# A four-layer graph network on one core: layer 2 by two levels of Strassen, its adjacency applied in PSUM, and weights fetched from DRAM in every turn

## The chip, the core and the metric

The kernel runs on one core of a Trainium2 chip. TensorE multiplies, with its results in PSUM; VectorE (DVE), ScalarE (ACT) and GpSimd (POOL) do the elementwise work; SP issues DMAs. All data are 32-bit floats. The metric is the time of one execution on the device in microseconds (us), as the median of the runs. Lower is better.

## The reference

There are 128 graphs of 128 nodes with 512 features, and a weighted adjacency matrix for each graph. Four layers follow each other, each of the form `x = layernorm(x + layer(x))`:

```python
# layer 0: A1 = A + I, normalised on both sides by d = rowsum(A1)**-0.5
out = relu(einsum('bnm,bmf,fc->bnc', An, x, kernel) + bias)
# layer 1: one weight for each node, from scores summed over the neighbours, softmax over the nodes
w = softmax(sum((q @ k.T) / 8 * adj, -1), axis=1);  out = w * v        # q, k, v = x @ W
# layer 2: W has 512 x 1024 elements, one half for x, one for the mean of the neighbours
agg = einsum('bij,bjf->bif', adj, x) / maximum(deg, 1e-6)
out = relu(einsum('bnf,of->bno', concatenate([x, agg], 2), W))
# layer 3: normalised A1 as in layer 0
out = An @ (x @ W + b)
```

## The kernel before

The work goes in 32 turns `t` of four graphs (`G = 4`, `NT = 32`). A product of the four graphs with a 512 x 512 weight is done by one level of Strassen: the rows are split by graph pairs `r` (graphs 0 and 2 against 1 and 3), the inner and the output dimension in halves, and the seven products are called B11, T1, T2, B21, B22, T3 and T4. Each weight tile holds its four blocks and the four sums that Strassen needs, made once at the start (`weight_sums`); the sums of the left operand are made each turn (`left_sums`, on GpSimd). `project` runs the seven products for one pair of graph rows after another, keeps partial results in PSUM banks that ScalarE copies between products (`copied`), and ends with `fin`, which adds onto `x` on VectorE. Its last product, T4, is put off as a *tail* (`finish_tails`) so that other work can stand before it.

A turn's path: `load`, `prep_rows` and `prep_turn` fetch the adjacency and make its two transposed forms `anT` (layers 0 and 3) and `arT` (layers 1 and 2). `l0_agg` multiplies x with `anT` (`aggregate`) and ScalarE copies the result to `agg0`; `l0_out` projects. `l1_turn` brings x, transposed, to `xT1`; `l1_out` makes v, q and k together (320 columns, tile `p_v`); `l1_scores`, `l1_softmax` and `l1_add` weigh v by graph: the weights come back to all partitions through a small TensorE transpose, `p_ws`, and VectorE then adds weighted v onto x. `l2_turn` brings the new x, transposed, to `xT2`; `l2_agg` multiplies x with `arT` to `agg2`; `l2_out` projects both halves, `xT2` with `w2x_sb` and `agg2` with `w2a_sb`, into the same products. `l3_agg`, `l3_bias` and `l3_out` end the turn, and `store` writes x.

The transposing (`turn_x`) in all turns but the first and the last goes through DRAM: four DMAs write x to a scratch tile (`xT2s` or `xT1s`), eight read it back in another order (`xT2y`, `xT1y`), and VectorE transposes blocks of 32 x 32. In the first and last turns TensorE transposes (`turn_on_tensor`). Normalisation is in `norm_stats`: mean and variance by VectorE's statistics instructions, the power -0.5 on GpSimd, and the scaling on ScalarE; layer 3 uses `norm_last`, in which ScalarE sums the values and their squares.

All the calls are recorded by `Plan`, and `emit` (line 323, the line that nearly every instruction of the profile shows) writes the instructions in the order that `schedule` chose. `estimate` gives each operation a duration, `Op.last` is its due time, found backwards from those that need it, and `run` lets each engine take the ready operation that is due first. TensorE keeps the order in which the calls were written, with `hooks` and `tails` to interleave them:

```python
        l0_out(t, {T2: [lambda: l2_agg(u, 0)], B21: [lambda: l2_agg(u, 1)]})
    tails.append(lambda: l1_turn(t))
    prep(t + 1)
    l2_out(u)
```

with `u = t - 1`: layers 0 and 1 of turn `t` run beside layers 2 and 3 of turn `u`. All weights stay in SBUF. SP issues the DMAs in one queue, in order.

Of the kernel before, what the change touches and what calls it, by code (L numbers as in the profile page):

```python
# [29 lines left out]
B11, T1, B21, B22, T2, T3, T4 = range(7)  # L30

# [95 lines left out]
class Plan:  # L127
# [8 lines left out]
    TRIALS = 100  # L136
# [62 lines left out]
    def schedule(self):  # L199
        number = {op: i for i, op in enumerate(self.ops)}  # L200
        for (_, tag, bufs), tiles in self.tags.items():
            used = []
            for t in sorted((t for t in tiles if t.ops), key=lambda t: number[t.ops[0]]):
                if len(used) == bufs:
                    old = used.pop(min(range(bufs), key=lambda i: number[used[i].ops[-1]]))
                    assert number[old.ops[-1]] < number[t.ops[0]], (tag, bufs)
                    for op in t.ops:
                        if op.preds.isdisjoint(t.ops):
                            op.preds.update(old.ops)
                used.append(t)  # L210
        now = 0
        for op in self.ops:
            assert all(number[p] < number[op] for p in op.preds)
            for p in op.preds:
                p.succs.append(op)
            if op.engine == "tensor":
                op.last = now
                now += op.dur
        for op in reversed(self.ops):
            due = min([s.last - self.hop(op, s) for s in op.succs], default=now)  # L220
            op.last = min(op.last, due - op.dur)
        done = self.run(number)
        tried = set()
        for _ in range(self.TRIALS):
            free, moves = 0, []
            for op in self.ops:
                if op.engine == "tensor":
                    gap, free = op.start - free, op.end
                    if gap > 100:
                        moves += [(-gap, number[op], n, op) for n in range(2)]  # L230
            moves = [m for m in sorted(moves) if m[1:3] not in tried]
            if not moves:
                break
            tried.add(moves[0][1:3])
            kept = [(op, op.start, op.end, op.after, op.last) for op in self.ops]
            self.press(moves[0][3], -moves[0][0], moves[0][2])
            again = self.run(number)
            if max(op.end for op in again) < max(c[2] for c in kept) - 20:
                done, tried = again, set()
            else:  # L240
                for op, start, end, after, due in kept:
                    op.start, op.end, op.after, op.last = start, end, after, due
        return done

    def press(self, op, gap, delay):


        while op.preds:
            late = max(op.preds, key=lambda p: p.end + self.hop(p, op))
            if delay and op.engine not in ("tensor", "sync"):  # L250
                ready = late.end + self.hop(late, op)
                for other in self.ops:
                    if other.engine == op.engine and other.start < op.start and other.end > ready + 20:
                        other.last = max(other.last, op.last + 100)
            op = late
            if op.engine == "tensor":
                break
            if not delay:
                op.last -= gap

    def run(self, number):
        queue = {e: [] for e in self.ENGINES}
        waiting = {op: len(op.preds) for op in self.ops}
        for op in self.ops:
            op.after = None
        free, bus, port, owner = dict.fromkeys(self.ENGINES, 0), 0, 0, None
        pe = [op for op in self.ops if op.engine == "tensor"]
# [4 lines left out]
        while len(done) < len(self.ops):  # L272
            best = None
            for e in self.ENGINES:
                q = queue[e]
                if e == "tensor":
                    q = [c for c in q if c[2] is pe[0]]
                if not q:
                    continue
                q = [(max(c[0], port if c[2].port else 0),) + c[1:] for c in q]  # L280
# [18 lines left out]
            if op.port:  # L299
                ready = max((p.end + self.hop(p, op) for p in op.preds), default=0)  # L300
                if e == "gpsimd" and owner is not None and owner.engine == "vector" and ready < port + self.CLOSE:
                    op.after = owner
                port, owner = op.end, op
# [4 lines left out]
            if e == "tensor":  # L308
                pe.pop(0)
            done.append(op)  # L310
            for s in op.succs:
                waiting[s] -= 1
                if not waiting[s]:
                    queue[s.engine].append((max(p.end + self.hop(p, s) for p in s.preds), number[s], s))
# [32 lines left out]
def estimate(engine, method, args, kw):  # L347
# [5 lines left out]
    if method == "dma_start":  # L353
        size = max(int(np.prod(v.shape)) if isinstance(v, bass.AP) else v.idx.size * 32 * len(v.quads) for v in args)
        return 470, Plan.LAND + size / 60, size, False
    if engine == "scalar":
        return (380 if method == "activation" else 160) + 0.83 * n, 0, 0, False
# [5 lines left out]
    return 160 + (1.12 if len(both) > 1 else 1.04) * n, 0, 0, len(both) > 1  # L363
# [3 lines left out]
def kernel(  # L367
# [19 lines left out]
    xp = Pool(nc, ctx.enter_context(tc.tile_pool(name="xp", bufs=4)), 4)  # L387
    ap = Pool(nc, ctx.enter_context(tc.tile_pool(name="ap", bufs=2)), 2)
    tp = Pool(nc, ctx.enter_context(tc.tile_pool(name="tp", bufs=4)), 4)
    sp = Pool(nc, ctx.enter_context(tc.tile_pool(name="sp", bufs=4)), 4)  # L390
# [23 lines left out]
    def weight(src, name, queue, turned=False):  # L414


        w = const.tile([P, 2, 7, H], FP, tag=name, name=name)
        for h in range(2):
            to = w[:, :, 2 * h:2 * h + 2].rearrange("p c j m -> p c (j m)")
            if turned:  # L420
                for b in range(Q):
                    queue.dma_start(to[b * K:(b + 1) * K], src.rearrange("(b h c k) m -> h b k c m", b=Q, h=2, c=2)[h][b])
            else:
                queue.dma_start(to, src.rearrange("(h c p) m -> h p c m", h=2, c=2)[h])
        return w

    def weight_sums(w, eng):
# [3 lines left out]
        eng.tensor_tensor(w[:, :, T4], w[:, :, B21], w[:, :, T2], ALU.subtract)  # L431

# [14 lines left out]
    w0_sb = weight(w0, "w0_sb", nc.sync)  # L447
# [12 lines left out]
    w2x_sb = weight(w2T[0:F, :], "w2x_sb", nc.sync, turned=True)  # L460
    w2a_sb = weight(w2T[F:2 * F, :], "w2a_sb", nc.sync)
    w3_sb = weight(w3, "w3_sb", nc.sync)
# [6 lines left out]
    def prep_rows(t):  # L469
# [3 lines left out]
        nc.vector.tensor_reduce(deg, a, AX.X, ALU.add)  # L473
        dh = sp.tile([P, G], FP, tag="dh", name=f"dh_{t}")
        nc.vector.tensor_scalar(dh, deg, 1.0, None, ALU.add)
        d = sp.tile([P, G], FP, tag="d", name=f"d_{t}")
# [12 lines left out]
    def prep_tiles(t):  # L489
        st["anT", t] = ap.tile([P, G, P], FP, tag="anT", name=f"anT_{t}", bufs=3)  # L490
        st["arT", t] = ap.tile([P, G, P], FP, tag="arT", name=f"arT_{t}", bufs=2)
# [92 lines left out]
    def project(name, t, parts, fin, hooks=None, after=lambda: None, pairs=(0, 1), seeds=None, fold=None):  # L584
# [14 lines left out]
        def product(p, k, fresh=False):  # L599
            with nc.unit():  # L600
                for q in pairs:
                    for i, (left_, w) in enumerate(parts):
                        for c in range(2):
                            nc.tensor.matmul(p[:, q - pairs[0], :], operand(left_, k)[:, q, c, :], w[:, c, k, :],
# [5 lines left out]
        def block(tag):  # L610
            return tp.tile([P, 2, H], FP, tag=tag, name=f"{tag}_{name}_{t}", bufs=2)[:, 0:n]
# [54 lines left out]
    def norm_last(name, t, r, pairs):  # L666

        z = st["x", t]
        qs = slice(pairs[0], pairs[-1] + 1)
        sm, nm, sq, rstd, nmr = (sp.tile([P, 2], FP, tag=f"last{i}", name=f"last{i}_{t}_{r}", bufs=2) for i in range(5))  # L670
        for q in pairs:
            row = tp.tile([P, F], FP, tag="row", name=f"row_{t}_{r}_{q}", bufs=1)
            nc.scalar.activation(row, z[:, 2 * q + r, :], AF.Copy, accum_out=sm[:, q:q + 1])
        nc.scalar.mul(nm[:, qs], sm[:, qs], -1.0 / F)
        for q in pairs:
            row = tp.tile([P, F], FP, tag="row", name=f"square_{t}_{r}_{q}", bufs=1)
            nc.scalar.activation(row, z[:, 2 * q + r, :], AF.Square, bias=nm[:, q:q + 1], accum_out=sq[:, q:q + 1])
        nc.gpsimd.tensor_scalar(rstd[:, qs], sq[:, qs], 1.0 / F, LN_EPS, ALU.mult, ALU.add)
        nc.gpsimd.tensor_tensor(rstd[:, qs], rstd[:, qs], nhalf[:, qs], ALU.pow)
        if (t, pairs[0]) != (last, 1):  # L680
            nc.gpsimd.tensor_tensor(nmr[:, qs], nm[:, qs], rstd[:, qs], ALU.mult)
        for q in pairs:
            zg = z[:, 2 * q + r, :]
            if (t, q) == (last, 1):
                nc.vector.tensor_scalar(zg, zg, nm[:, q:q + 1], rstd[:, q:q + 1], ALU.add, ALU.mult)
            else:
                nc.scalar.activation(zg, zg, AF.Identity, bias=nmr[:, q:q + 1], scale=rstd[:, q:q + 1])
            if t == last:
                nc.sync.dma_start(out[t * G + 2 * q + r], zg)

    def norm_stats(name, t, r, pairs):
        if name == "o3" and (t, r, pairs[-1]) != (last, 1, 1):
            return norm_last(name, t, r, pairs)
# [10 lines left out]
        mr = sp.tile([P, 2], FP, tag="mr", name=f"mr{name}_{t}_{r}")  # L704
# [8 lines left out]
        nc.gpsimd.tensor_tensor(mr[:, qs], mv[:, qs, 0], rstd[:, qs], ALU.mult)  # L713
        nc.scalar.mul(nmr[:, qs], mr[:, qs], -1.0)
# [160 lines left out]
    def l2_agg(t, r):  # L875
        if r == 0:
            left("agg2", t)
# [152 lines left out]
```

## Time and profile before

| | |
|---|---|
| median of 3 runs | 2443.24 us (2443.18 to 2443.28) |
| profiled execution | 2442.89 us, its span 2441.1 us |
| granted TensorE clock | 0.999 |
| DMA traffic | 238.88 MB in the hardware queue, 37.5% of 16 engines' time |

Busy time of each engine, its share of the span, and what it is made of:

| engine | busy us | share | largest groups |
|---|---|---|---|
| TensorE | 2426.6 | 99% | products of layers 0 and 3 (`p_o<-w_sb`), of layer 2 (`w2x_sb`, `w2a_sb`), of layer 1 (`p_v`), aggregations (`p_agg`) |
| VectorE | 1365.1 | 56% | statistics 246, additions onto x, transposes of blocks |
| ScalarE | 1212.1 | 50% | copies of `p_agg` 227, scaling of x |
| GpSimd | 1156.4 | 47% | sums of left operands, powers |

One line of a group reads: line, engine, operation, output and input tiles, shapes, count, then busy us, mean ns of one, and idle time before them with what ended it. The granted clock is the share of full speed that the throttle let TensorE have. The chain of waits is followed back from the last instruction: each step names what released it.

### The profile page before, as it was taken

How to read it: one execution, taken by the hardware profiler on the slowest of the kernel's cores; microseconds unless marked ns; L12 is line 12 of the kernel's file. 1: busy time of each engine (PE TensorE's matmuls, PEld its weight loads, DVE VectorE, ACT ScalarE, POOL GpSimd, SP SyncE). 2: the span in 40 equal slices, each digit the busy share in tenths (PEclk: the TensorE clock that was granted, in tenths of full speed). 3: DMA queues.
4: the chain of work that ended last, by engine and by line, in shares of the span. 5: the costliest groups of instructions: out<-in, count | busy, mean ns of one | idle time of the engine just before them, and what ended most of it. 6: DMA issues, size and time to landing. Idle time of an engine off the chain costs nothing.

```text
span 2441.1 us, 35406 instructions
## 1 busy us (share of the span) xinstructions
PE 2426.6 (99%) x12460; PEld 2088.7 (86%) x12460; DVE 1365.1 (56%) x2847; ACT 1212.1 (50%) x2569; POOL 1156.4 (47%) x1516
## 2 busy tenths in 40 slices
PE   9999999999999999999999999999999999999998
PEld 7888888888888888888888888888888888888887
DVE  5655655555555655656565555556555555655545
ACT  5444544555445454455544554444555445454445
POOL 5353545545454444544444553545445454444442
PEclk9999999999999999999999999999999999999999
DMA  5243333443434434244333444343442434433220
GB/s 177 51 107 95 77 105 103 118 114 73 112 87 125 117 74 104 84 124 117 90 88 99 110 117 108 76 108 94 122 120 66 112 82 126 117 81 97 61 78 35
DMA packets 393264, 241.14 MB, mean 99 GB/s; under 512 B 140416, under 2 KB 358016, under 8 KB 393088
## 3 DMA queue, kind: packets, MB, share of 16 engines
q1 hardware_dynamic: 393088, 238.88, 37.5%
q8 instruction: 99, 1.62, 0.3%
q14 instruction: 77, 0.63, 0.1%
HBM read 126.62 MB, written 112.20 MB: 98 GB/s over the span
## 4 chain that ended last, share of the span: by engine, by line
PE 97%; POOL 1%; DVE 1%; ACT 1%; issue 0%; DMA 0%; POOLq 0%; ACTq 0%; DVEq 0%
PE p_o L323 63%; PE p_v L323 19%; PE p_agg L323 14%; PE p_sc L323 1%; DVE x L323 0%; POOL xT1s L323 0%; POOL w_sb L323 0%; ACT xT L323 0%; ACT agg L323 0%; PE p_ws L323 0%; PE p_w L323 0%; ACT x L323 0%; DMA ana<-in_adj_dram 0%; POOL w2a_sb L323 0%; ACT xT2y L323 0%
## 5 line engine op out<-in xcount | busy, mean ns | idle before, releaser
L323 PE MATMUL p_o<-w_sb,agg 128*128 128x256 f32 x2048 | 476.8, 380 | 0.8 <-DVE x L323 0.5
L323 PEld LDWEIGHTS p_o<-w_sb,agg 128*128 128x128 f32 x2048 | 381.6, 190 | 51.7 <-DVE x L323 0.9
L323 ACT COPY agg<-p_agg 128x512 f32<-128x512 f32 (+1 forms) x415 | 226.7, 554 | 376.6 <-PE p_agg L323 376.6
L323 DVE SCALAR_TENSOR_TENSOR x<-p_o,x 128x512 f32<-128x512 f32 (+1 forms) x130 | 88.7, 683 | 405.2 <-PE p_o L323 402.4
L323 PE MATMUL p_v<-wv_sb,xT 128*128 128x320 f32 x1024 | 307.2, 433 | 0.0
L323 PE MATMUL p_o<-w2x_sb,xT 128*128 128x256 f32 x1024 | 263.1, 379 | 0.5 <-ACT xT L323 0.5
L323 PE MATMUL p_o<-w2a_sb,agg 128*128 128x256 f32 x1024 | 262.8, 379 | 0.0
L323 PEld LDWEIGHTS p_agg<-anT,x 128*128 128x128 f32 x2048 | 243.6, 192 | 11.8 <-DVE anT L323 0.4
L323 PEld LDWEIGHTS p_v<-wv_sb,xT 128*128 128x128 f32 x1024 | 189.7, 190 | 71.2 <-issue 0.2
L323 PE MATMUL p_agg<-anT,x 128*128 128x128 f32 x2048 | 244.2, 275 | 0.2 <-DVE anT L323 0.2
L323 ACT COPY p_o<-p_o 128x512 f32<-128x512 f32 (+1 forms) x196 | 110.7, 565 | 255.8 <-PE p_o L323 255.8
L323 PE MATMUL p_v<-wv_sb,xT1s 128*128 128x320 f32 x768 | 228.3, 433 | 1.1 <-POOL xT1s L323 1.0
L323 PEld LDWEIGHTS p_o<-w2x_sb,xT 128*128 128x128 f32 x1024 | 194.2, 190 | 30.5 <-ACT xT L323 1.0
L323 PEld LDWEIGHTS p_o<-w2a_sb,agg 128*128 128x128 f32 x1024 | 194.6, 190 | 26.5
L323 ACT ACTIVATE x<-x,nmro,rstdo 128x512 f32<-128x512 f32 x256 | 198.0, 808 | 4.1
L323 PE MATMUL p_o<-w2x_sb,xT2s 128*128 128x256 f32 x768 | 197.3, 379 | 2.0 <-DVE xT2s L323 2.0
L323 PE MATMUL p_o<-w2a_sb,agg2s 128*128 128x256 f32 x768 | 197.1, 379 | 0.0
L323 PEld LDWEIGHTS p_v<-wv_sb,xT1s 128*128 128x128 f32 x768 | 145.6, 190 | 59.5 <-POOL xT1s L323 2.6
L323 PE MATMUL p_o<-w_sb,agg0s 128*128 128x256 f32 x768 | 176.4, 379 | 0.0
L323 POOL TENSOR_TENSOR xT1s<-xT 128x512 f32<-128x512 f32 x32 | 40.7, 1273 | 277.4 <-DVE xT L323 250.4
L323 PE MATMUL p_o<-w_sb,agg3s 128*128 128x256 f32 x744 | 171.2, 379 | 0.6 <-POOL agg3s L323 0.6
L323 DVE BATCH_NORM_STATS2 bno<-x 128x6 f32<-128x512 f32 x258 | 164.8, 679 | 3.4
(143 smaller groups left out, 4024.3 us busy)
## 6 DMA issues: line engine op xcount, KB each, us to landing
x<-in_x_dram SPq DMA_DIRECT2D x31, 1024.0 KB, 5.4
out_dram<-x SPq DMA_DIRECT2D x31, 1024.0 KB, 5.7
xT2s<-x SPq DMA_DIRECT2D x120, 256.0 KB, 2.5
xT2y<-xT2s SPq DMA_DIRECT2D x240, 128.0 KB, 3.4
xT1s<-x SPq DMA_DIRECT2D x120, 256.0 KB, 2.5
xT1y<-xT1s SPq DMA_DIRECT2D x240, 128.0 KB, 3.4
sa<-ana SPq DMA_DIRECT2D x120, 128.0 KB, 3.1
ya<-sa SPq DMA_DIRECT2D x120, 128.0 KB, 3.9
```

Source lines behind the costliest of these rows:

```text
L323: op.ins = getattr(getattr(self.nc, op.engine), method)(*[v.real() if isinstance(v, Ref) else v for v in args], **{k: v.real() if isinstan ...
```

## The change

**Layer 2.** Instead of aggregating x first, the kernel multiplies x with both halves of the weight, as one 512 x 1024 product, by two levels of Strassen: 7 x 7 products of one matmul each (128 rows, 128 inner, 256 columns). The first level is over pairs of graphs, inner chunks and columns within a half; the second over graph rows, inner halves and the two halves of W. The sums of the left operand are made by `l2_turn` and `inner_sums` (two of them on VectorE as the transposes arrive, the others mostly on GpSimd). The products go in four passes (`PASSES`), interleaved by `AT`; each pass collects into `v` (the x half) and `y` (the half to be aggregated) on VectorE and ScalarE. Then, for each graph, ScalarE copies `v` into a PSUM bank, one matmul of 512 columns with `arT` adds the aggregated `y` onto it (`p_2g`), and VectorE adds the positive part to x, with the sum over features as a by-product. `l2_agg` and `l2_both` are gone.

**Weights.** Four tiles `wb_sb`, `wa_sb`, `wc_sb` and `wz_sb` hold layer 2's weights and sums; `wz_sb` is also the place of the weights of layers 0 and 3. Their three versions are written to DRAM at the start (`keep`) and fetched in seven pieces each, three times in a turn (`fetch`); each piece waits until the products that read the one before it are done.

**Normalisation.** Layers 1 and 2 take their means from the by-products of the additions, and the squares on ScalarE (`norm_last`), instead of VectorE's statistics. Layer 0 makes `nmr` in one VectorE instruction for one of GpSimd and one of ScalarE.

**Buffers.** x has three buffers for four, the left operands and small tiles three for four, `arT` three for two.

**Order.** The search over `press` is gone. `run` now also lets TensorE choose by due time, gives buffers out as it goes, and takes two tables that are written out in the file: `EARLY` shifts the due time of operations named by engine, tile and number within a turn (366 entries), and `MOVED` names operations that go to another engine (`move`): additions between VectorE and GpSimd, copies and scalings from ScalarE to VectorE.

```diff
+PASSES = (B11,), (B21, T2), (T1, T3), (B22, T4)
+AT = 0, 0.5, 7, 9
...
-            due = min([s.last - self.hop(op, s) for s in op.succs], default=now)
-            op.last = min(op.last, due - op.dur)
...
+            due = min([s.last - self.hop(op, s) for s in op.succs + then[op]], default=now)
+            op.last = min(op.last, due - op.dur) - 100 * EARLY.get(keys[op], 0)
+        return self.run(number)
...
-                if e == "tensor":
-                    q = [c for c in q if c[2] is pe[0]]
+                q = [(r,) + c[1:] for c in queue[e] for r in (ready(c[0], c[2]),) if r is not None]
...
-    xp = Pool(nc, ctx.enter_context(tc.tile_pool(name="xp", bufs=4)), 4)
+    xp = Pool(nc, ctx.enter_context(tc.tile_pool(name="xp", bufs=3)), 3)
...
+    def fetch(name):
+        def piece(k):
+            nc.sync.dma_start(wz_sb[:, k], st[name, "kept"][:, k])
+
+        for k in ORDER[:-1]:
+            piece(k)
...
-        nc.gpsimd.tensor_tensor(mr[:, qs], mv[:, qs, 0], rstd[:, qs], ALU.mult)
-        nc.scalar.mul(nmr[:, qs], mr[:, qs], -1.0)
+        nc.vector.scalar_tensor_tensor(nmr[:, qs], mv[:, qs, 0], -1.0, rstd[:, qs], ALU.mult, ALU.mult)
...
+            def product(p, k, fresh=False):
+                with nc.unit():
+                    for i, j in enumerate(js):
+                        nc.tensor.matmul(p[:, i], ops[j][k], w[:, k, i], start=(fresh and i == 0), stop=True,
+                                         skip_group_check=True)
...
+                p = ps_b.tile([P, F], FP, tag="pb", name=f"p_2g_{t}_{g}")
+                nc.scalar.copy(p, v[:, r, q].rearrange("p i m -> p (i m)"))
+                nc.tensor.matmul(p, st["arT", t][:, g, :], y[:, r, q].rearrange("p i m -> p (i m)"), start=False, stop=True,
+                                 skip_group_check=True)
+                nc.vector.scalar_tensor_tensor(z[:, g, :], p, 0.0, z[:, g, :], ALU.max, ALU.add,
+                                               accum_out=st["sm", t][:, 2 * r + q:2 * r + q + 1])
...
-            l0_out(t, {T2: [lambda: l2_agg(u, 0)], B21: [lambda: l2_agg(u, 1)]})
+            fetch("w0d")
+            l0_out(t)
...
+        fetch("w2d")
         tails.append(lambda: l1_turn(t))
         prep(t + 1)
         l2_out(u)
+        fetch("w3d")
+        l1_out(t, {})
         if t < last:
             l0_agg(t + 1)
-        l1_out(t, {})
+        finish_tails()
+        l1_scores(t)
         l3_agg(u)
-        l1_scores(t)
+        l1_softmax(t)
         l3_bias(u)
-        l3_out(u, {B11: [lambda: l1_softmax(t)], T2 if t < last else T1: [lambda: l1_add(t)]})
-        if t < last:
-            l2_turn(t)
-
-    l2_both(last, 0)
...
+        l3_out(u, {B11: [lambda: l1_add(t)]})
+        l2_turn(t, turn_x if t < last else turn_on_tensor)
+
+    fetch("w2d")
+    l2_out(last)
+    fetch("w3d")
```

In TensorE's built order, the layer-2 products of turn `u` stand among those of layer 0 of turn `t`, and the four `p_2g` among the first products of layer 1. The fetches of layer 0's pieces begin while layer 3 still runs; piece T4 stands on SP's queue between `xT2s` and `xT2y`, piece B22 behind the eight `xT2y`.

## The prediction

> **What bounds the kernel now.** I read the page first, then the chain that ended last in order of time, the waits of TensorE, the groups by form, the timeline of one turn, and the DMA rows. The page: its first part, then the slices.
>
> ```profile
> span 2441.1 us, 35406 instructions
> PE 2426.6 (99%) x12460; PEld 2088.7 (86%) x12460; DVE 1365.1 (56%) x2847; ACT 1212.1 (50%) x2569; POOL 1156.4 (47%) x1516
> ...
> PEclk9999999999999999999999999999999999999999
> DMA  5243333443434434244333444343442434433220
> ```
>
> TensorE is busy 99% at a granted clock of 0.999, every other engine about half. Between 200 and 2300 us it waits for nobody; the whole list of its waits comes to under 10 us, all at the two ends. Its longest lines (who, for whom, us in all, times, longest):
>
> ```profile
> PE p_o L323 <- DVE xT2s L323: 2.0, 2, 1.6
> PE p_warm L323 <- POOL ident masks.py:199: 1.3, 1, 1.3
> PE p_agg L323 <- ACT x L323: 1.0, 2, 0.7
> ```
>
> So the time is the sum of the matmuls, and one turn of four graphs repeats every 75.26 us. The chain gives the price of a matmul pass (start, length, what, how many; the trace has two MATMUL passes for each fp32 matmul of the kernel):
>
> ```profile
> 517.75 25.90 PE p_o L323 x120
> 551.76 12.92 PE p_v L323 x48
> ```
>
> A pass of 256 columns takes 25.90/120 = 0.2158 us and one of 320 columns 12.92/48 = 0.2692, so 0.000834 us per column more. A 128-column aggregation pass takes 0.111 (sixteen from 1042.60 to 1044.38 in the timeline).
>
> **What the change takes from TensorE.** Layer 2 had per turn 7 products x 8 matmuls = 56 of 256 columns (112 passes, 24.17 us) and 16 aggregation matmuls (32 passes, 3.56 us): 27.73. It now has 7 x 7 = 49 matmuls of 256 columns (98 passes, 21.15 us) and 4 of 512 columns that put the adjacency on. No row has 512 columns; the line through 256 and 320 gives 0.4294 a pass, twice the 256 row 0.4316; I take the first: 8 passes, 3.44. Together 24.59, so 3.15 us less per turn, 100.7 us in 32 turns (the other end costs 0.6 us). All of it lies on the path. The profiled execution took 2442.89 us (span 2441.1 and 1.8 around it; the median of the runs is 2443.24): 2442.9 - 100.7 = 2342 us if TensorE stays as dense. The rest asks whether it does. Positions below are TensorE's instructions in the built order, added up by these prices.
>
> **The path from layer 1 to layer 2.** In both kernels x is normalised after `l1_add`, written to DRAM (`xT2s`), read back (`xT2y`), transposed on VectorE, and multiplied. Before, the weighted sum's broadcast `p_ws` stands 21.0 us of matmuls ahead of the first layer-2 product, with VectorE idle 1.7 to 1.9 us for the DMA and TensorE fed just in time. The timeline of one such hand-over:
>
> ```profile
> 584.63 4.02 SPq L323 DMA_DIRECT2D xT2s<-x  x4
> ...
> 588.75 4.16 SPq L323 DMA_DIRECT2D xT2y<-xT2s  x8
> ...
> 592.96 1.86 SPq L323 DMA_DIRECT2D ya<-sa  x4
> ...
> 593.88 1.30 DVE L323 STREAM_TRANSPOSE xT<-xT2y 128x512 f32<-128x512 f32 x2 [1.85 <-DMA xT2y<-xT2s]
> ```
>
> From the first `xT2y` issue to the transposes it takes 5.1 us. In the changed order only 36 matmuls of 256 columns and `p_ws` itself stand between `p_ws` and the first layer-2 product: 15.5 + 0.2 = 15.75 us. The chain, from `p_ws`: to VectorE 0.3 (as `p_w` to `mn`); `ws` 0.15; four additions with an accumulator, 0.75 + 0.08 each (the 512-wide `x<-b_sb,rs,x` row and the accumulator row), and two small means 0.16: 3.64; the fold of layer 3, 1.84; two additions onto x 0.68 each; one normalisation 0.55: 7.8. The other half (squares 0.91 each and a copy on ScalarE, POOL 1.1, normalise 0.81) is ready by then. Then two `xT2s` issues 0.6, landing 2.5: 10.9. SP has meanwhile issued the other two and the fetch of weight piece T4, which stand ahead. `xT2y` to transposes 5.1, transpose 0.69, five to six handovers of 0.05: 17.0. That is 1.2 us more than 15.75, so TensorE waits 1.2 us a turn where it waited for nothing; 0.5 if the fold runs as fast as its quickest case (1.22 at 2384 us), 2.4 if the two DMAs land 0.6 us later each, well inside their spreads (2.3 to 5.0 us). The chain is paid by 30 turns: 36 us.
>
> **Other new waits.** These I cost at nothing, with what covers them:
> - Weights fetched in turn: 21 pieces of 256 KB a turn, 56 DMAs on SP for 35 (56 issues of 0.43 to 0.53 us are 24 to 30 us of a turn). The rows:
>
> ```profile
> x<-in_x_dram SPq DMA_DIRECT2D x31, 1024.0 KB, 5.4
> ...
> xT2y<-xT2s SPq DMA_DIRECT2D x240, 128.0 KB, 3.4
> ...
> ana<-in_adj_dram SPq DMA_DIRECT2D x32, 256.0 KB, 5.9
> ...
> out_dram<-x SPq DMA_DIRECT2D x4, 256.0 KB, 2.0
> ```
>
> A piece lands after 2.0 to 5.9 us. From 1024 against 256 KB one takes about 1.1 us of the DMA engines, 24 us a turn on top of 0.40 x 75 = 30. The tightest turn-around is B11 from layer 3 to layer 0: 7.1 us of matmuls, less 0.9 for the end of the product and the issue, leaves 6.2: covered at both ends. Piece B22 is issued on SP behind the eight `xT2y`, at 10.9 + 8 x 0.53 = 15.1 after `p_ws`, lands at 17.1 to 18.5 (by the `xT2y` row) and is wanted at 18.3 without the 1.2 us wait, 19.5 with it: covered by that wait, 0.2 without.
> - Layer 0 to layer 1 (`xT1`): from the last layer-0 product to the T1 product of layer 1 there were 25 us and are 16.6. The chain: to VectorE 0.25, relu-add 0.69, statistics 1.9, POOL 1.1, a small multiplication 0.25, two additions queued ahead and the normalisation 1.7, issue and landing of `xT1s` 2.6, `xT1y` to transposes 5.1, two transposes 1.4, POOL's sum 1.3, handovers 0.2: 16.5. Nothing, or 0.7 over where the landings are 0.8 later.
> - Layer 2's output: from the last `p_2g` to `p_agg3`: to VectorE 0.45, relu-add 0.83, mean 0.16, four squares 3.64, POOL 1.4, normalise 0.81, handovers 0.3: 7.6 us under 8.8 of matmuls. x in three buffers for four: store 5.7 and load 5.4 under 13.2.
> - VectorE goes from 1365.1/32 = 42.7 us a turn to some 60 (108 instructions by their nearest rows), POOL falls from 36 to 32, ScalarE rises from 38 to 43. Between the last layer-0 product and the first `p_2g`, TensorE has 20.3 us of work, and VectorE must do 19.0 in it: 16 instructions of 512 elements at 0.68, three of 1024 at 1.22, five of 256 at 0.42, eight smaller of 2.3 in all. By the fold's 1.84 for the three it is 20.8, 0.5 too much.
>
> Here a rule speaks against the change. The groups by form have the fold and two additions of equal size (last columns: count, busy us, mean ns, idle before them):
>
> ```profile
> L323 DVE TENSOR_TENSOR x<-x,f_o 128x1024 f32<-128x1024 f32 x31 | 56.6, 1827 | 10.6 <-ACT f_o L323 10.5
> ...
> L323 DVE TENSOR_TENSOR ana<-ana,ident 128x512 f32<-128x512 f32 x32 | 47.4, 1482 | 0.0
> ...
> L323 DVE TENSOR_TENSOR ana<-ana,d 128x512 f32<-128x512 f32 x32 | 22.1, 690 | 73.2 <-POOL d L323 73.1
> ```
>
> `ana<-ana,ident` has a minimum of 0.66 and a median of 1.67 us, and the fold takes 1.84 with POOL at work against 1.22 with POOL idle. The Trainium skill, SBUF — State Buffer, section Who interferes with whom, says that a VectorE instruction with two SBUF inputs contends with a GpSimd instruction that reads SBUF, and whoever comes second waits for the whole instruction. The rows agree with it. By the rule alone, with every new two-input addition meeting one of POOL's, the sum would be that of the second rival; by the rows, with POOL idle more than half the time, it stays at 2392.
>
> **Ends.** Now no other work covers the last layer-2 output: TensorE waits the 7.6 us above once. Turn 0 and the last turn have their combining steps uncovered (fold-sized and 0.68 us additions, some 2 us each), and the begin loads and sums weights in place (0 to 10, I take 3). Together 7.6 + 2 + 2 + 3, about 14; from 8 to 22.
>
> Sum: 2342 + 36 + 14 = 2392 us.
>
> **Rivals.**
> 1. Nothing waits in the steady turns (chance 0.28). For: in the old kernel the same hand-overs run just in time for thirty turns. Against: the 5.1 us of DMA don't shrink, and the distance did by 5 us. 2342 + 14 = 2356; with the shortest ends 2350.
> 2. VectorE becomes the bound, slower (0.17). The place is the stretch between the last layer-0 product and `p_2g`: six VectorE additions there have two SBUF inputs. If each waits 0.62 to 1.01 us for POOL as the rows above do, that is 3.7 to 6.1 less the 1.3 to spare, 2.4 to 4.8 a turn besides the 1.2: 2342 + 14 + 30 x 3.6 = 2464 or more. It decides from (2448 - 2342 - 14)/30 = 3.1 us of waits a turn. For: VectorE at five sixths, its queue in order. Against: POOL is busy under half the time, and has less to do.
> 3. The matmuls don't get fewer as counted, because accumulating into a copied bank costs passes. The order shows 49 and 4 per turn, and `p_o<-p_o` copies are followed by passes of the same 0.2158 today. I give it nothing apart.
>
> **Numbers.** Forecast 0.50, rival 1 0.28, rival 2 0.17, an end within 0.2% of 2443 (2438 to 2448, about what a measurement can tell from no change) 0.05. Faster: 0.50 + 0.28 = 0.78. The forecast's own range, 0.5 to 2.4 us a turn, is 2371 to 2428. The range, 2350 (rival 1 with the shortest ends) to 2448, leaves out rival 2 and little else.
>
> **What would show it.** Right: MATMUL passes of `p_2x` of 0.216 us and of `p_2g` of 0.43; a turn of about 73.3 us; one wait of about 1.2 us a turn of TensorE for VectorE's `xT`, behind `xT2y`; fetches of `wz_sb` never named in TensorE's waits; 7 to 8 us idle after the last `p_2g`. Wrong: waits named for `wz_sb` DMAs (then the fetch is the price); waits of `p_2g` or `p_v` on VectorE of over 2 us a turn (rival 2); a turn of 72.1 us (rival 1).

## The result, and the profile after

| | before | changed |
|---|---|---|
| median | 2443.21 us (2443.00 to 2443.28, 4 runs) | 2505.49 us (2500.74 to 2513.68, 4 runs) |
| ratio | | 1.0259, 95% interval 1.0231 to 1.0287 |
| profiled execution | 2442.89 us | 2503.64 us, its span 2501.8 us |

The change costs 62 us where 51 less were forecast. A turn takes 76.5 us (median of the turns 2 to 30, from one `p_ws` to the next), where 73.3 were forecast and 75.26 were needed before. The changed kernel's runs also spread over 13 us, those of before over 0.3.

The page, first part and slices, where before TensorE was busy 99% and the DMA engines about 0.4:

```profile
span 2501.8 us, 36164 instructions
PE 2387.3 (95%) x11244; PEld 1936.1 (77%) x11244; DVE 1928.2 (77%) x3901; ACT 1284.7 (51%) x2744; POOL 1086.7 (43%) x1470
...
DMA  6366655665655666556656566565666655665542
```

TensorE has the fewer passes that the change promised (11244 for 12460), VectorE the 60 us a turn that the prediction counted (1928.2/32), and the DMA engines are half as busy again. TensorE's list of waits (who, for whom, us in all, times, longest), under 10 us before, now begins so:

```profile
PE p_2x L448 <- DVE xT L448: 54.6, 29, 4.1
PE p_2x L448 <- POOL xT2s L448: 16.9, 24, 1.1
PE p_agg L448 <- ACT x L448: 6.9, 1, 6.9
PE p_2x L448 <- POOL xT L448: 6.1, 29, 0.3
...
PE p_o L448 <- DMA wz_sb<-w0d: 1.6, 4, 0.8
```

Three quarters of it (77.6 us of some 105) is layer 2's products waiting for their left operand; the weight fetches (`w0d`) are named for 1.6 us. One hand-over in the timeline (start, length, engine, what; in brackets the idle time before and what ended it):

```profile
1054.03 0.27 PE L448 MATMUL p_ws<-ident,e_sb 128*128 128x128 f32 x1
...
1061.24 0.32 SPq L448 DMA_DIRECT2D wz_sb<-w2d  x1
1061.61 2.49 SPq L448 DMA_DIRECT2D xT2s<-x  x4
1064.20 1.18 SPq L448 DMA_DIRECT2D wz_sb<-w0d  x1
1065.84 4.18 SPq L448 DMA_DIRECT2D xT2y<-xT2s  x8
1070.12 0.38 SPq L448 DMA_DIRECT2D wz_sb<-w0d  x1
...
1071.72 1.30 DVE L448 STREAM_TRANSPOSE xT<-xT2y 128x512 f32<-128x512 f32 x2 [2.29 <-DMA xT2y<-xT2s]
...
1072.49 0.70 PE L448 MATMUL p_2x<-wb_sb,xT 128*128 128x256 f32 x2 [2.06 <-DVE xT L448]
...
1073.06 0.42 DVE L448 TENSOR_TENSOR inner<-xT 128x256 f32<-128x256 f32 x1
...
1074.48 1.30 DVE L448 STREAM_TRANSPOSE xT<-xT2y 128x512 f32<-128x512 f32 x2 [0.99 <-DMA xT2y<-xT2s]
...
1075.95 0.73 POOL L448 TENSOR_TENSOR inner<-inner,xT 128x256 f32<-128x256 f32 x1
1076.02 0.95 DVE L448 TENSOR_TENSOR inner<-xT 128x256 f32<-128x256 f32 x1
...
1078.03 0.72 POOL L448 TENSOR_TENSOR xT2s<-xT2s,xT 128x256 f32<-128x256 f32 x1 [1.34 <-DVE inners L448]
...
1078.80 0.70 PE L448 MATMUL p_2x<-wb_sb,xT2s 128*128 128x256 f32 x2 [0.87 <-POOL xT2s L448]
```

From `p_ws` to the first product of layer 2 it takes 18.46 us here (mean of the turns 2 to 30: 18.29). TensorE waits for the first half of `xT2y` (2.06), then for a sum made from the second half (0.87). That sum, GpSimd's second `xT2s`, starts only behind VectorE's sums into `inner` and `inners`; the `inner<-xT` that runs beside GpSimd's own sum takes 0.95 us, the one before it alone 0.42. The fetch rows (us from issue to landing) beside those of the round trip:

```profile
wz_sb<-w0d SPq DMA_DIRECT2D x210, 256.0 KB, 3.4
...
xT2s<-x SPq DMA_DIRECT2D x120, 256.0 KB, 3.5
xT2y<-xT2s SPq DMA_DIRECT2D x240, 128.0 KB, 4.1
```

Before, `xT2s` landed in 2.5 us and `xT2y` in 3.4.

To see all that TensorE lost, I took from the trace the step from each pass to the next, less the usual step of that tile (0.216 us for `p_o` and `p_2x`, 0.269 for `p_v`, 0.429 for `p_2g`), wherever it was more than 0.03 us, and added it up by place, in us:

| | before | changed |
|---|---|---|
| all steps at their usual length | 2418.1 | 2319.2 |
| turns: first product of layer 2 | 0 | 59.4 |
| turns: second wait (sums from the second half, `xT2s`, `inner`) | 0 | 21.9 |
| turns: third wait (`xT`, after a GpSimd sum) | 0 | 11.2 |
| turns: many of 0.05 to 0.26 (0.104 behind each wait; operands just in time) | 1.9 | 30.8 |
| turns: clock at half | 0 | 13.0 |
| turns: others | 0.7 | 4.1 |
| begin and end | 12.4 | 34.0 |
| sum | 2433.1 | 2493.6 |

The passes saved 98.9 us, and 159 us of lost time came with them.

### The profile page after: what moved, and what is told of

The parts are those of the page before. It is cut to its first block, busy times and chain, and to the rows that moved or that the text cites. A ratio compares the mean times of both kernels' runs of the same rounds, so it can differ in the third digit from the quotient of the medians.

```text
span 2501.8 us, 36164 instructions
## 1 busy us (share of the span) xinstructions
PE 2387.3 (95%) x11244; PEld 1936.1 (77%) x11244; DVE 1928.2 (77%) x3901; ACT 1284.7 (51%) x2744; POOL 1086.7 (43%) x1470
## 2 busy tenths in 40 slices
DMA packets 490431, 417.40 MB, mean 167 GB/s; under 512 B 151808, under 2 KB 373504, under 8 KB 489856
## 5 line engine op out<-in xcount | busy, mean ns | idle before, releaser
L448 PE MATMUL p_o<-wz_sb,agg 128*128 128x256 f32 x2048 | 465.5, 379 | 2.5 <-ACT p_o L448 1.5
L448 PEld LDWEIGHTS p_o<-wz_sb,agg 128*128 128x128 f32 x2048 | 386.2, 190 | 56.0 <-ACT p_o L448 1.9
L448 ACT ACTIVATE square<-x,last1o 128x512 f32<-128x512 f32 x255 | 184.4, 723 | 61.6 <-DVE last1o L448 57.3
L448 PE MATMUL p_o<-wz_sb,agg0s 128*128 128x256 f32 x768 | 194.0, 397 | 7.6 <-DVE p_o L448 3.5
L448 PEld LDWEIGHTS p_o<-wz_sb,agg0s 128*128 128x128 f32 x768 | 148.9, 198 | 42.8 <-DVE agg0s L448 14.1
L448 PE MATMUL p_o<-wz_sb,agg3s 128*128 128x256 f32 x744 | 177.3, 383 | 1.0 <-issue 0.6
L448 ACT ACTIVATE x<-x,last4o,last3o 128x512 f32<-128x512 f32 x191 | 145.2, 808 | 53.3 <-POOL last4o L448 53.3
L448 DVE TENSOR_TENSOR y<-p_2x,y 128x512 f32<-128x512 f32 (+1 forms) x256 | 155.1, 615 | 7.8 <-PE p_2x L448 3.2
L448 PEld LDWEIGHTS p_o<-wz_sb,agg3s 128*128 128x128 f32 x744 | 136.4, 190 | 30.8 <-POOL agg3s L448 11.7
L448 POOL TENSOR_TENSOR xT<-xT 128x256 f32<-128x256 f32 (+1 forms) x128 | 134.9, 1054 | 56.9 <-DVE y L448 34.9
```

The costliest lines, as they stand in the source:

```text
L448: op.ins = getattr(getattr(self.nc, op.engine), method)(*[v.real() if isinstance(v, Ref) else v for v in args], **{k: v.real() if isinstan ...
```

## The experiments

Theory A: the hand-over from layer 1 to layer 2 is too short for its round trip through DRAM. Theory B: the weight fetches are the price. Theory C: VectorE is the bound. In all kernels but the last the order of the instructions is that of the changed kernel, apart from what is shown or said, so that nothing else is rearranged: the edits act in `emit`, on the list that `schedule` gave (`n` holds the tiles' names of the operation).

### Without fetches, without the round trip, with less for VectorE

No fetches:

```diff
+            if op.engine == "sync" and n[0] == "wz_sb" and n[1] in ("w0d", "w2d", "w3d"):
+                continue
```

> Leaves out every later fetch of the weights (all 21 pieces of 256 KB in each turn); the products use whatever wz_sb held first, so layers 0, 2 and 3 multiply by the wrong weights. The order of every other instruction is that of the changed kernel. Theory A, the hand-over from layer 1 to layer 2 is too short for its transfers: the transfers from xT2s over xT2y to the transposes take 5.57 us with the fetches and took 5.13 us before, so at most some 0.5 us a turn comes back at each of the two waits behind them, 2470 to 2495 us. Theory B, the fetch is the price (its traffic, or SP standing behind it): the waits of 3 us a turn and what follows them go, 2350 to 2400 us. Theory C, VectorE is the bound: nothing changes, 2495 to 2510 us.

Transposes that read x itself:

```diff
+            if op.engine == "vector" and op.calls[0][0] == "transpose" and n[1] in rows:
+                method, args, kw = op.calls[0]
+                op.calls = [(method, (args[0], rows[n[1]].pop(0).rearrange("p a (c j) -> p a c j", c=C)), kw)]
```

> VectorE's transposes for layer 2 read x itself in place of xT2y, so they wait for no transfer; xT2s and xT2y are still moved, with all their traffic. Left out is the exchange between partitions, so layer 2 gets its x wrongly turned. Theory A: the first wait of a product of layer 2 (59 us in all), the two behind it (21 and 11 us) and most of the small restarts and of the halved clock behind them go, 2360 to 2400 us. Theory B: the traffic is still there and finds the next transfer that is late, 2440 to 2500 us. Theory C: VectorE has the same work, 2480 to 2510 us.

Fewer VectorE sums:

```diff
+            if op.engine == "vector" and n[0].startswith("y2_") and n[2].startswith("y2_") and op.calls[0][1][0].idx.size == 4 * H:
+                continue
```

> Leaves out three VectorE additions a turn in layer 2's output (the 1024-column sums into y2 that add one block of y2 onto others, 1.22 + 2 x 1.40 = 4.0 us of VectorE a turn), so layer 2's second part of the output lacks terms; everything else is as in the changed kernel. Theory A: the waits are ahead of these additions, 2490 to 2505 us. Theory B: 2490 to 2510 us. Theory C: up to 4.0 us a turn come back, 2385 to 2440 us.

Both of the first two edits:

> The edits of the two runs that leave out the fetches and the round trip, together (wrong weights, and x of layer 2 wrongly turned). Theory A: what the fetches cost apart from the round trip is nothing, so it is within 10 us of the run that leaves out the round trip alone. Theory B: it is 60 us or more under that run. Theory C: 2480 to 2510 us.

| | us | against before | against changed |
|---|---|---|---|
| no fetches | 2431.23 | 0.9949 (0.9935 to 0.9964) | -74.3 |
| no round trip | 2473.89 | 1.0123 (1.0108 to 1.0138) | -31.6 |
| less for VectorE | 2506.27 | 1.0266 (1.0249 to 1.0283) | +0.8 |
| neither fetches nor round trip | 2408.03 | 0.9856 (0.9841 to 0.9871) | -97.5 |

Theory C falls: 3.8 us a turn less on VectorE (1808.1 us busy for 1928.2) brought nothing. Theory A falls in the form I gave it: it had expected little from the fetches and most from the round trip. Theory B's ranges hold the second and the fourth run; the first lies between A and B, so the fetches are the larger price, but with them gone the change is still worth only 12 us of its 98.9. The rows of the kernel without fetches, and the first line of TensorE's waits:

```profile
xT2s<-x SPq DMA_DIRECT2D x120, 256.0 KB, 2.8
xT2y<-xT2s SPq DMA_DIRECT2D x240, 128.0 KB, 3.2
```

```profile
PE p_2x L455 <- POOL xT2s L455: 21.5, 31, 1.4
```

Without the fetches `xT2y` is issued 10.76 us after `p_ws` and the first transposes start at 15.49 (means of the turns 2 to 30; changed: 11.86 and 17.52). The round trip ends 2.0 us earlier, TensorE's products cover it, and the first wait shrinks from 59.4 to 2.1 us in all; no half clock is left in the turns. The second wait stays (25.9). So the fetches cost through the transfers that they delay, not through a wait for themselves. That is also why taking the round trip away alone gave only 32 us: the next line in order was then the fetch itself. TensorE's waits without the round trip begin with

```profile
PE p_o L459 <- DMA wz_sb<-w0d: 46.9, 29, 2.5
```

1.6 us a turn, ahead of layer 0's product B22, whose piece is issued behind the eight `xT2y`. In the changed kernel the first wait had covered it.

### Bytes or the queue, and which fetches

A quarter of each piece, at the same places with the same waits of SP:

```diff
+            if op.engine == "sync" and n[0] == "wz_sb" and n[1] in ("w0d", "w2d", "w3d"):
+                method, args, kw = op.calls[0]
+                op.calls = [(method, tuple(v[:, 0:1, 0:128] for v in args), kw)]
```

> Every fetch is still issued at its place on SP with its waits, but each moves a quarter of its piece, 64 KB in place of 256 KB (so three quarters of each piece keep old weights and the products are wrong). Theory B1, the fetches' bytes are under way beside xT2s and xT2y and make these land later: near the run without fetches (2431 us), 2431 to 2450 us. Theory B2, it is SP, which stands in line behind TensorE's products before each fetch may be issued, with xT2s and xT2y queued behind it: near the changed kernel, 2485 to 2505 us.

2441.38 us (0.9993, 0.9983 to 1.0003): 64 of the 74 us are the bytes under way; 10 are left for the quarter and the issues. It is not the number of packets: the page counts 490431 DMA packets here as in the changed kernel. `xT2s` lands in 2.8 us and `xT2y` in 3.2, as without fetches.

Three of the 21 fetches moved on SP:

```diff
+        order = self.later(order, {("w0d", T4), ("w2d", B11)}, r"xT2y_\d+_1")
+        order = self.sooner(order, {("w0d", B22)}, r"xT2y_\d+_0")
```

> The changed kernel with the whole computation; on SP alone three of the 21 fetches of a turn change places: w2d B11 (was ahead of xT2s) and w0d T4 (was between xT2s and xT2y) go behind the last xT2y, and w0d B22 (was behind the last xT2y) goes between the two halves of xT2y. The bytes are the same. Theory B1 in the narrower form, what counts is which fetches are under way in the 8 us of the round trip: two fetches fewer in front bring xT2y forward by some 1 us, and most of the first wait (2.0 us a turn) goes without w0d B22 taking its place, 2440 to 2470 us. Theory B3, the bytes cost the same wherever they lie: 2490 to 2510 us.

2479.78 us (1.0147, 1.0131 to 1.0164): 25.7 less than the changed kernel, with the same bytes. That lies between the two expectations: the place counts, but the gain is smaller than I thought. The first wait went (59.4 to 5.9 us in all) and the second grew from 21.9 to 54.7, since with B22 between them the second half of `xT2y` still came late: its transposes start 19.29 us after `p_ws`, against 18.11 without fetches.

The same with the sum that waits moved up on GpSimd (`xT2s2` directly behind `xT2s1`):

> The run with the three moved fetches, and on GpSimd one more step: xT2s2 (the sum that the second waiting product of layer 2 reads) is issued directly behind xT2s1, ahead of the sum into inner, and no longer held back until VectorE's two sums into inner are through. The whole computation is there. In the run without fetches that product still waited 0.84 us a turn, 25 us in all, for this sum, which began 1.3 us after GpSimd was free. Expected if that is what the second wait hangs on: 15 to 25 us under the run with the moved fetches alone, if VectorE and GpSimd do not slow each other by as much: then within 5 us of it.

2477.34 us (1.0150, 1.0132 to 1.0169). The wait only changed its name, as the first lines of the two kernels show, moved fetches first:

```profile
PE p_2x L493 <- POOL xT2s L493: 40.3, 31, 1.4
```

```profile
PE p_2x L499 <- POOL inner L499: 38.2, 30, 2.2
```

That is the expectation's second case, gained 2.4 us of the 15 to 25, and its condition is met too: moved beside each other, the sums of the two engines slow each other. VectorE's `inner<-inner,xT` and `inners<-inner` take 0.83 us each for 0.42 before the move, GpSimd's second `xT2s` 0.93 for 0.73 and its `inner<-inner,xT` 0.90 for 0.73 (medians of the turns 2 to 30). So the second wait hangs on the second half's arrival and on all the sums behind it, not on their order alone.

### Half of the hand-over by TensorE

In turns 2 to 30 the two `xT2s` and four `xT2y` transfers of row 1 and VectorE's two transposes of it are not issued; in their places stand, for each graph `q` (the second one's transposes and copy in two parts):

```diff
+                out.append(new("scalar", ("copy", (y[:, q].rearrange("p c (b j) -> p c b j", b=Q),
+                                                   z.rearrange("p b (c j) -> p c b j", c=C)))))
...
+                    pieces.append(new("tensor", *[("transpose", (p[:, c, :], y[:, q, c], ident)) for c in cs]))
+                    copies.append(new("vector", ("tensor_copy", (x[:, 2 * q + 1, cs[0]:cs[-1] + 1], p[:, cs[0]:cs[-1] + 1]))))
```

> The changed kernel with the whole computation, but in turns 2 to 30 half of the hand-over from layer 1 to layer 2 (row 1, two graphs) goes through TensorE: two copies by ScalarE, eight transposes of 128 columns ahead of the product T2 of layer 0 (8 x 0.109 = 0.87 us a turn, 25 us in all), and copies back by VectorE in place of its transposes. xT2s and xT2y of row 1 are no longer moved, which takes 2 x 256 KB and 4 x 128 KB a turn out of the round trip. Theory A with the fetches beside it, the round trip is too long for the products that cover it: the first wait (59 us), w0d B22's lateness behind it and part of the second (21 us) go, less 25 us for the transposes, 2425 to 2460 us. Rival, what is late there is the sums on VectorE and GpSimd whatever brings x: the first wait turns into the second, 2475 to 2510 us.

2445.45 us (1.0010, 1.0001 to 1.0019), 60 us less than the changed kernel although TensorE has 25 us more to do; the rival's range is far off. First, second and third wait are 14.3, 8.5 and 12.1 us. The run also takes 1 MB a turn of transfers away, and the half that still makes the round trip lands sooner (`xT2y` in 2.6 us for 4.1), so it doesn't tell how much came from the missing half and how much from less traffic beside the other.

With the moves as well:

```diff
+        order = self.later(order, {("w0d", T4), ("w2d", B11)}, r"xT2y_\d+_0")
...
+            if keys[order[i]] == "g:xT2s2:0":
+                j = max(order.index(p) for p in order[i].preds)
+                order[i].after = None
+                order.insert(j + 1, order.pop(i))
+        for i in [i for i, op in enumerate(order) if keys[op] == "v:y1:0"]:
...
+                order.insert(j[0], order.pop(i))
```

> The run with row 1 on TensorE, and with it the moves of the earlier runs: w0d T4 and w2d B11 behind the last xT2y, xT2s2 directly behind xT2s1 on GpSimd, and on VectorE the copy of the first product of layer 2 into y1 behind the three sums into inner, which stood behind it. The whole computation is there. If each of the waits at the hand-over has its own cause, all three go: 2400 to 2430 us, under the kernel before (2443 us). If the third wait (10 us) and the restarts grow in their place: 2430 to 2450 us.

2433.79 us (0.9959, 0.9944 to 0.9974), 72 us less than the changed kernel and the only whole computation under the kernel before. The hand-over is then nearly gone from TensorE's list, whose first lines are

```profile
PE p_2x L559 <- POOL xT L559: 9.8, 29, 0.3
PE p_agg L559 <- ACT x L559: 6.9, 1, 6.9
```

First and second wait are 1.9 and 3.1 us, the third 14.6 (12.1 without the moves), so the time lies in the range of the expectation's second, lesser case, though the third wait grew by only 2.5 us.

### The same traffic in the kernel before

```diff
+                self.copies({("xT2s_0", "xT2s_1"): 2, ("xT2s_1", "xT2y_0"): 1, ("xT2y_1", "ya"): 7, ("xT1s_0", "xT1s_1"): 1,
+                             ("xT1y_1", ""): 6, ("x", "sa"): 4}.get((last, n), 0))
```

> The kernel before, with the whole computation, and beside it 21 transfers of 256 KB a turn that nobody reads, from the weights in memory to memory, at places in SP's order like those of the fetches (four ahead of xT2s, two between its halves, one between xT2s and xT2y, seven behind xT2y, one between the halves of xT1s, six behind xT1y). Theory: the price of the fetches is that the round trip of the changed kernel has no spare time; before, its first transposes lie 2.4 us ahead of the first product of layer 2, so the same traffic costs little, 2443 to 2460 us. Rival: traffic of this size costs its 60 to 75 us in any kernel, 2495 to 2520 us.

2557.19 us (1.0469, 1.0452 to 1.0487): over both expectations. TensorE's waits:

```profile
PE p_v L339 <- ACT p_v L339: 62.9, 50, 3.9
PE p_v L339 <- DVE v L339: 11.9, 23, 0.5
PE p_o L339 <- DVE xT L339: 6.1, 8, 1.2
```

At the hand-over to layer 2 it went as I thought: the first transposes came 1.6 us later (20.13 for 18.53 us after `p_ws`, medians), the first product stayed at 20.95, and that place cost 6 to 8 us in all. The price arose in layer 1. Its first product still started 47.0 us after `p_ws` (medians of both kernels), although the copies behind `xT2y` had held SP, so that `ya` was issued 23.2 us after `p_ws` (17.6 before) and `xT1s` 34.1 (30.8). But the adjacency of the next turn (`ana`), behind six more copies, was issued at 48.4 and landed at 55.9, for 41.1 and 47.0 before. VectorE's `deg` waited for it, ScalarE's `dmn` for VectorE, and the copies of `p_v` that TensorE waits for came only behind `dmn`:

```profile
ACT dmn L339 <- DVE dm L339: 220.5, 29, 10.2
DVE deg L339 <- DMA ana<-in_adj_dram: 147.4, 30, 6.9
```

Before, `deg` waited 3.4 us for `ana` in all. The copies also landed in 5.0 us, from memory to memory, where the fetches took 3.1 to 3.4, so the size cannot be carried over to the changed kernel. What the run shows is that traffic of this size can cost far more than the hand-over it was placed at: the price is set by the transfers that it delays, and by what stands in line behind them.

## Why the prediction was wrong

The forecast was 2342 us of dense work, 36 of waits and 14 at the ends. Step by step:

- **TensorE's passes: right.** 0.216 us for `p_2x`, 0.429 for `p_2g` (estimated 0.4294), and 98.9 us saved for 100.7.
- **Fetches at nothing: the step that failed.** Each piece was held against the products that wait for it, and by that measure it was covered. But the 21 pieces were not put into the price of the transfers beside them: `xT2s` was taken at 2.5 us, `xT2y` to transposes at 5.1, as in the trace of before, while the fetches of layer 0's pieces, `w2d` B11 and T4 lie just there. The run without fetches is 74 us faster, the quarter fetch 64. The prediction did name the row (0.6 us later for each DMA, "well inside their spreads") but only as the end of a range. Its own test, "fetches never named in TensorE's waits", came out but for 1.6 us and still pointed the wrong way.
- **The hand-over: the place right, partly by luck.** The wait of `p_2x` for VectorE's `xT` behind `xT2y` was forecast at 1.2 us a turn, and is 2.0. The distance was right (without fetches the first product starts 16.24 us after `p_ws` at the earliest, for 15.75 and two short restarts), and so were the steps up to `xT2s` (7.59 for 7.8 us). The rest of the chain was taken at 9.2 us from there (17.0 - 7.8) and took 10.7; without fetches at most 9.0. So the chain as it was priced, with transfers that nothing slows, gives almost no wait (2.1 us in all without fetches, for 36 forecast): the 1.2 us came from a chain taken at 17.0 us that needs 16.3 at most and a distance taken at 15.75 that is 16.24, and the 2.0 us that are there come from the fetches.
- **What follows the first product: left out.** I priced one wait. The second half of `xT2y` and the sums on VectorE and GpSimd gave a second (21.9), GpSimd's later sums a third (11.2). The small ones (28.9 more than before) were not priced either. Without fetches the second and the third wait still cost 36 us and the small ones some 26, which is why that run lies 39 us over the forecast although the first wait is gone.
- **B22 covered by the first wait: right**, as the run without the round trip shows. But when that cover is gone it costs 46.9 us, 1.6 a turn, not the 0.2 that the prediction left uncovered.
- **Layer 0 to layer 1, and x in three buffers at nothing: right by the list of waits.** `xT1s` is named for 1.0 us in all, x only at the end. No run tested either.
- **Ends: 14 forecast, 21.6 measured;** the one wait behind the last `p_2g` was forecast at 7.6 us and is 7.1 (`p_agg` for ScalarE's `x`, 6.9 in the list).
- **Rival 2, VectorE: the right side for a wrong reason.** The fold and the wide new additions of the groups by form:

```profile
L448 DVE TENSOR_TENSOR y<-u,y 128x1024 f32<-128x1024 f32 x64 | 89.6, 1401 | 1.2
...
L448 DVE TENSOR_TENSOR x<-x,f_o 128x1024 f32<-128x1024 f32 x31 | 37.7, 1217 | 0.0
```

The fold runs at 1.22 us, not the 1.84 of before, and leaving out the wider sums changed nothing. The rule weighed in the prediction (the Trainium skill, SBUF — State Buffer, Who interferes with whom) agrees with these rows, but its cost lies elsewhere. At the fold of the hand-over above GpSimd is idle. On the way to the second wait it is not: there VectorE's second `inner<-xT` takes 0.95 us beside GpSimd's sum and the first 0.43 (medians), an estimated 0.5 us a turn of that chain, and in the run with `xT2s2` moved up such sums took longer again.

Another rule points to the fetches. The Trainium skill, DMA: Bandwidth & Descriptors, section Queues, rings and completion order, says that all DMAs issued by SP go through one row of rings on the same DMA engines, and that an engine consumes descriptors in ring order. The runs agree: `xT2y` behind fewer fetched bytes landed sooner (3.2 us without them, 4.1 with), and moving two fetches from ahead of it to behind it (and a third between its halves) brought the first transposes from 17.52 to 15.60 us after `p_ws`. No run tells the order in the rings from a sharing of the DMA engines or the memory.

**Open.** Of the 78.6 us that TensorE still loses in the fastest kernel with the whole computation, 36 lie at the ends and 14.6 in the third wait; no run took these apart. What makes the third wait, and the operands that arrive just in time (`agg3s`, `agg0s`), is read from the trace alone.

## What to carry to other kernels

A transfer that nobody waits for still has a price: put its bytes into the landing time of every transfer under way beside it, above all of a round trip whose covering work the same change shortens. When a wait is taken away, ask at once what is late next at that place; here the fetch itself and the sums from the second half stood behind the first wait, and of the kernels with the whole computation only the one with all the moves beat the old kernel. A test for "the fetch is the price" must look at the delayed transfers, not only at waits that name the fetch.

## What was not expected of the hardware

Short waits halved the clock. In the changed kernel's turns from 200 us on there are six stretches at half the granted clock, five of 3.41 us and one of 6.83, and each lies at a wait of TensorE of 1.9 to 4.1 us; in four other turns waits of 2.1 to 2.7 us had none. All such stretches in the turns cost 13 us in steps twice as long, and may be part of the spread between runs (granted clock 0.994 in the fastest run, 0.989 in the slowest). In the turns of the kernel before and of the run without fetches there is none.

What divides the waits is where they fall. In every trace with more than one, the starts of these stretches lie whole multiples of 3.413 us apart (the six at 763.47, 841.97, 920.48, 1606.56, 1763.57 and 2070.77 us: 0, 23, 46, 247, 293 and 383 of them from the first). Laid out on that grid, TensorE's idle time is 1.90 us or more in the window just before each of the six, and at most 1.82 us in every other window of these turns; the longer waits without half clock were split between two windows. In all traces together, from 200 to 2350 us, half clock followed every window with more than 2.0 us idle and none with less than 1.89.

The Trainium skill, TensorE: Matmul & The Clock Gate, Part 1, gives windows of 3413 ns, run freely, and the half clock after an idle window of some 3.4 us. The windows agree; by the idle time the traces differ, since about 1.9 us within one window was enough, so the measurement decides.
